# Six transformer layers on one core: when the next layer's weights and tables are fetched, Newton's temporaries in PSUM, and the order of k's transfers

## The chip, the core and the metric

The kernel runs on one core of a Trainium2 chip. Its engines work side by side and in their own order: PE (TensorE, matmuls; PEld is its weight loading), DVE (VectorE), ACT (ScalarE), POOL (GpSimd, which works on SBUF only here) and SP (SyncE, which issues the DMAs). SBUF is the working memory; PSUM is the small memory that matmuls write, in banks of 512 floats per partition. The metric is the time of one execution in microseconds of the device. Three runs of the kernel before gave 3605.53, 3603.47 and 3618.85 us, median 3605.53.

## The reference

The input has 16 sequences of 256 tokens with 128 features, all float32. First a plain causal attention with 16 heads of 8 is added to x. Then come six layers (the Stack), whose result is added to x:

```python
for i in range(DEPTH):                     # 6
    x = attn_layer(shift_tokens(x), Wqkv[i], q_scale[i], k_scale[i], Wo[i]) + x
    x = ffn_layer(shift_tokens(x), ln_g[i], ln_b[i], W1[i], b1[i], W2[i], b2[i]) + x
```

`attn_layer` has 16 heads of 64. It projects q, k and v, normalizes q and k of each head to length 1 and scales them, turns them by rotary tables that also carry a power of the position, and attends in windows: each window of 32 queries sees its own 32 keys and the 32 before, with a mask. `ffn_layer` is a layer norm, a product with W1 (128 x 682), one half times the gelu of the other, and a product with W2 (341 x 128). `shift_tokens` moves half of the features by one token.

## The kernel before

The first stage computes the plain attention and its residual in about 390 us; nothing of it is changed. The second stage is the Stack. All activations stay in SBUF as `yT`, features on partitions and two sequences of 256 tokens side by side. One step n = 16 l + s is layer l with sequence s, so n runs from 0 to 95. Each step is written as two halves, u = 0 and u = 1, for the first and second half of the heads, and in one half the pieces of several steps are interleaved:

- of step n + 2: q and k are projected by `proj_qk` (L484 to L504) for group g of four heads, k = 0 for q and 1 for k. Two matmuls (L497) write one PSUM bank, ACT squares it (L498, `sq`), and DVE multiplies it with the rotary table `ab` (L499, `t`, 128 x 1024). POOL adds the squares (`add_sq`, L509) and the turned halves (`add_t`, L515, `tq`).
- of step n + 1: `norms` sums squares by matmul, `roots` (L530 to L547) transposes the sums into PSUM (`nT`, L533) and DVE takes the inverse square root of 128 x 64 numbers: a lower bound (L537, `nx`), a first guess by an integer trick (L541, `rn`), and three Newton rounds of three instructions (L544 to L546, temporaries `nz`). POOL spreads the result (`spread_rn`, L552, `kb`), PE transposes it into PSUM (`spread_k`, L563, `bc`), DVE multiplies k by it (`norm_k`, L577), and SP sends q and k of two groups to `us` (L579): per group, one transfer for each u.
- of step n: `masks` writes the mask into the PSUM tile `simt` with one ACT copy of 128 x 1024 (L604), `sim` adds the scores with 128 matmuls (L617), `soften` scales them and takes the maximum on DVE (L629, L637), `below` subtracts it on POOL (L643, `sm`), `power` is the exponential on ACT (L648, `ex`). `proj_v` (L587) makes v, ACT copies it to `vn` (L593) and SP sends shifted copies to `vs` (L594, L596).
- of the half before: `share` and `divide_by` make the weights sum to one (L655, L656; L664 on POOL, and on DVE for the second part of the first heads), `attn_T` transposes them (L670, L672, `aT`), `attn_v` multiplies with v (L690), `evict` copies the result (L701).
- of step n - 1: `project_out` multiplies with Wo (L712) and DVE adds to `yT` (L717). The feed-forward part of a pair of steps is spread over four halves.

`ORDER` names the pieces of the four kinds of half (even or odd step, u = 0 or 1), and `in_order` pins the sequence of instructions on PE, DVE, ACT and POOL to it. The order of DMAs on SP is the planner's: it puts a load into the queue as soon as its buffer is free. Small PSUM tiles come from one pool of four banks (`psum1`); the planner gives out the banks. The tiles `wqk` (one for each g), `wv`, `wout`, `w1`, `w2` exist once; `ab` and the tag `t12` have two buffers, `tq` six.

Weights are asked for at a layer's first use of them: `proj_qk` with s == 0 and k == 0 calls `load_qk` (L429) and, for g == 0, `load_tables`, which fetches the rotary table (L437) and multiplies it with the layer's scales by two POOL instructions of 128 x 1024 (L439). They stand in POOL's order at this place, the piece Q0a of the half with n + 2 = 16 l and u = 0, behind SM0 and SM1 (L664) and ahead of QA0 (L509), QT0 (L515), SB0, SB1 (L643) and KB (L552). `proj_v`, `project_out` and `glu_part` call `load_v`, `load_out` and `load_glu` in the same way.

Of the kernel before, what the change touches and what calls it, by code (L numbers as in the profile page):

```python
# [7 lines left out]
F32 = mybir.dt.float32  # L8
# [30 lines left out]
def tile_transformer(  # L39
# [347 lines left out]
    with ExitStack() as st:  # L387
# [59 lines left out]
        def load_v(l):  # L447
            W["v"] = wpool.tile([P, 2, NG, 2, DH], F32, tag="wv", name=f"wv_{l}")
            src = f_wqkv[l][:, 2 * INNER :].rearrange("p (g u y) -> p u g y", g=NG, u=2)
            for u in range(2):  # L450
                nc.sync.dma_start(W["v"][:, u].rearrange("p g x d -> p g (x d)"), src[:, u])

        def load_out(l):

            w = wpool.tile([P, 2, 4, E], F32, tag="wout", name=f"wout_{l}")
            for x in range(2):
                for g in range(2):
                    nc.sync.dma_start(
                        w[64 * x : 64 * x + 64, g],
                        f_wo[l].rearrange("(g x i d) e -> g x d i e", g=2, x=2, i=4, d=DH)[g, x],  # L460
                    )
            W["out"] = w

        def load_glu(l):
            w1 = wpool.tile([P, 2 * DI], F32, tag="w1", name=f"w1_{l}")
            nc.sync.dma_start(w1, f_w1[l])
            w2 = wpool.tile([P, 3, E], F32, tag="w2", name=f"w2_{l}")
            for i, (a, n) in enumerate(DI_PARTS):
                nc.sync.dma_start(w2[:n, i, :], f_w2[l][a : a + n, :])
            W["1"], W["2"] = w1, w2  # L470

        xs, sq2s, t12s, sq, tq, us, rn, kbs, ao, exs, aTs, pos, xns, hs = ({} for _ in range(14))
# [11 lines left out]
        def proj_qk(n, g, k):  # L484

            l, s = divmod(n, NSEQ)
            if s == 0 and k == 0:
                load_qk(l, g)
                if g == 0:
                    load_tables(l)  # L490
            if k == 0:
                sq2s[n, g] = e2.tile([P, 2, 2, S], F32, tag="sq2", name=f"sq2_{n}_{g}")
                t12s[n, g] = e2.tile([P, 2, 2, 2, S], F32, tag="t12", name=f"t12_{n}_{g}")
            sq2, t12 = sq2s[n, g], t12s[n, g]
            ps = psum1(f"qk_{n}_{g}_{k}")
            for t in range(2):
                nc.tensor.matmul(ps[:, t * S : t * S + S], W["qk", g][:, k, t, :], xs[n], start=True, stop=True)  # L497
            nc.scalar.activation(sq2[:, k].rearrange("p t n -> p (t n)"), ps, AF.Square)  # L498
            nc.vector.tensor_tensor(  # L499
                t12[:, k].rearrange("p f t n -> p f (t n)"),  # L500
                ps.unsqueeze(1).to_broadcast([P, 2, 2 * S]),
                W["ab", l][:, k].rearrange("p f t n -> p f (t n)"),
                ALU.mult,
            )  # L504
# [25 lines left out]
        def roots(n, n2):  # L530
            ps = psum1(f"nT_{n}").rearrange("p (h g m) -> p h g m", h=4, g=4)
# [4 lines left out]
            x = p2.tile([P, 2, NG, 8], F32, tag="nx", name=f"nx_{n}")  # L536
            nc.vector.tensor_scalar(x, ps[:, 0:2, :, 0:8], 1e-24, None, ALU.max)  # L537

            y = p3.tile([P, 2, NG, 8], F32, tag="rn", name=f"rn_{n}")
            x_, y_ = (v.rearrange("p h g m -> p (h g m)") for v in (x, y))  # L540
            nc.vector.tensor_scalar(y_.bitcast(I32), x_.bitcast(I32), -0.5, 1597463007.0, ALU.mult, ALU.add)  # L541
            for _ in range(3):
                z = p4.tile([P, 64], F32, tag="nz", name=f"nz_{n}")
                nc.vector.tensor_tensor(z, x_, y_, ALU.mult)  # L544
                nc.vector.scalar_tensor_tensor(z, z, -0.5, y_, ALU.mult, ALU.mult)
                nc.vector.scalar_tensor_tensor(y_, z, 1.5, y_, ALU.add, ALU.mult)  # L546
# [20 lines left out]
        def norm_k(n, j):  # L567
# [4 lines left out]
            ps = bcs.pop((n, j))  # L572
            for a in range(2):
                g = 2 * j + a
                t4 = tq.pop((n, g))
                k = t4[:, :, 1]
                nc.vector.tensor_tensor(k, k, ps[:, a].unsqueeze(1).to_broadcast([P, 2, S]), ALU.mult)  # L577
                for u in range(2):
                    nc.sync.dma_start(us[n, u][:, g], t4[64 * u : 64 * u + 64])  # L579

        def proj_v(n, u, c):

            l, s = divmod(n, NSEQ)
            if u == 0 and c == 0 and s == 0:
                load_v(l)
            ps = psum1(f"v_{n}_{u}_{c}")
            nc.tensor.matmul(  # L587
                ps, xs[n][:, P * c : P * c + P], W["v"][:, u].rearrange("p g x d -> p (g x d)"), start=True, stop=True
            )
            v, w = vn[u], vs[u]  # L590
# [7 lines left out]
        def masks(n, u):  # L598

            if n == 0 and u == 0:  # L600
                for x in range(2):
                    nc.tensor.matmul(simt[:, x], ident_b, mask_s, start=True, stop=True, skip_group_check=True)
            else:
                nc.scalar.copy(simt, mask_s.unsqueeze(1).to_broadcast([P, 2, 512]))  # L604
# [54 lines left out]
        def divide_by(n, i):  # L659
# [3 lines left out]
            on = nc.vector if i == 1 else nc.gpsimd  # L663
# [39 lines left out]
        def project_out(n, u):  # L703

            l, s = divmod(n, NSEQ)
            if s == 0 and u == 0:
                load_out(l)
            a = ao.pop((n, u))
            ps = psum1(f"wo_{n}_{u}")
            for j in range(4):  # L710
                g, x = divmod(j, 2)
                nc.tensor.matmul(  # L712
                    ps[:, :S].rearrange("p (h m) -> p h m", h=2), W["out"][:, g, 2 * u + x, :], a[:, x, :, g, :],
                    start=(j == 0), stop=(j == 3)
                )
            y = yT[s // 2][:, (s % 2) * S : (s % 2 + 1) * S].rearrange("p (a h m) -> p h a m", a=2, h=2)
# [85 lines left out]
        def glu_part(mm, i):  # L802
            l, b, _, w, name = which(mm)
            if b == 0 and i == 0:
                load_glu(l)
# [11 lines left out]
            hs[mm, i] = h  # L817

        def glu_out(mm):
            l, b, c0, w, name = which(mm)  # L820
            ps = psum1(f"w2_{name}")[:, :w]
# [3 lines left out]
            nc.vector.scalar_tensor_tensor(y, ps, vecs[:, l, V_B2 : V_B2 + 1], y, ALU.add, ALU.add)  # L825

# [25 lines left out]
        def sums(n):  # L852
# [3 lines left out]
            (0, 0): "SH0 SM0 SH1 SM1 S0 S1 Q0a Q0b QA0 QT0 NS S2 S3 SO0 SB0 SO1 SB1 WO RT KB AT0 AT1 V0 AV0 AC0 MK Q1a GP2 Q1b QA1 QT1 SK0 NK0 PW0 PW1 AV1 AC1 V1",  # L856
            (0, 1): "SH0 SM0 SH1 SM1 S0 S1 Q0a Q0b QA0 QT0 SK1 NK1 S2 S3 SO0 SB0 SO1 SB1 WO SHF GS AT0 AT1 V0 AV0 AC0 MK Q1a Q1b QA1 QT1 PW0 PW1 AV1 AC1 GO V1",
            (1, 0): "SH0 SM0 SH1 SM1 S0 S1 Q0a Q0b QA0 QT0 NS S2 S3 SO0 SB0 SO1 SB1 WO RT KB AT0 AT1 V0 AV0 AC0 MK GC Q1a GV Q1b QA1 QT1 GT SK0 NK0 PW0 PW1 AV1 AC1 V1",
            (1, 1): "SH0 SM0 SH1 SM1 S0 S1 Q0a Q0b QA0 QT0 SK1 NK1 GN S2 S3 SO0 SB0 SO1 SB1 WO SHF AT0 AT1 V0 AV0 AC0 MK Q1a GP0 GP1 Q1b QA1 QT1 PW0 PW1 AV1 AC1 V1",
        }  # L860

        def half(n, u):
# [16 lines left out]
            def roots_of(n):  # L879
# [5 lines left out]
                "SM0": lambda: do(b, divide_by, bi),  # L885
                "SM1": lambda: do(b, divide_by, bj),
# [14 lines left out]
                "RT": lambda: do(n + 1, roots_of),  # L901
                "SK0": lambda: do(n + 1, spread_k, 0),
# [15 lines left out]
                "MK": lambda: do(*((n, masks, 1) if u == 0 else (n + 1, masks, 0))),  # L918
# [12 lines left out]
            if n == N - 1 and u:  # L931
                what["WO"] = lambda: (do(n - 1, project_out, u), glu_shift((N // 2 - 1, 0)))
# [3 lines left out]
        def tail():  # L936
# [5 lines left out]
            for i in (2, 3):  # L942
                share(n, i)
                divide_by(n, i)
# [4 lines left out]
            project_out(n, 0)  # L949
            for i in (2, 3):  # L950
# [5 lines left out]
            project_out(n, 1)  # L956
            glu_shift(z)
# [122 lines left out]
```

## Time and profile before

| | |
|---|---|
| median of three runs | 3605.53 us |
| the profiled execution, by the device | 3608.32 us |
| its span, first to last instruction | 3606.5 us |
| mean granted TensorE clock | 0.989 |
| DMA queue q1: packets, MB | 248060, 321.14 |
| L499 `t`, DVE | 768 of 1217 ns |
| L439 `ab`, POOL | 12 of 1896 ns |
| L604 mask, ACT | 191 of 1022 ns |
| L544, L545, L546 (Newton), DVE | 288 each, mean 478, 333, 230 ns |
| L541 (first guess), DVE | 96, mean 415 ns |

How to read it: the profile records one execution. Busy time is the time in which an engine has an instruction at work; "idle before" is the time the engine stood still ahead of an instruction, with the event that ended it. `out<-in` names tiles without buffer numbers: `qk`, `nT`, `bc`, `v`, `hg`, `ha`, `cen` and others are PSUM tiles of the pool of four. A wait is put down to the last event before the instruction, so a name may be that of a neighbour. PEclk is the granted clock of TensorE, 1.00 being full speed.

### The profile page before, as it was taken

To read this page: it belongs to the slowest core of one execution; us is meant where nothing else is said; L and a number is where in the kernel's file an instruction comes from. 1 tells how busy PE (TensorE), PEld (TensorE's weight loads), DVE (VectorE), ACT (ScalarE), POOL (GpSimd) and SP (SyncE) were. 2 spreads that over 40 slices of the span, in tenths; PEclk is the share of its full clock that TensorE was granted. 3 is DMA by queue.
4 is the path that set the end of the run, shared out by engine and by line. 5 is a ranking of instruction groups with operands and counts; after the bars stand their busy time and mean duration, and the time that the engine had idled before them with its cause. 6 is when DMAs were issued, how large, how long until landed. Compare 5 with 4: busy or idle time off the path is not lost.

```text
span 3606.5 us, 151183 instructions
## 1 busy us (share of the span) xinstructions
PE 3435.6 (95%) x66566; PEld 2405.9 (67%) x66567; DVE 2840.4 (79%) x4876; ACT 2031.6 (56%) x3377; POOL 2576.9 (71%) x2730
## 2 busy tenths in 40 slices
PE   7999699999999999999999999999999999999997
PEld 6777466666666666666666666666666666666665
DVE  5665788887888887877887888887888888888784
ACT  3444355655665655655655655655656565565554
POOL 2221788777777787777777777777787877777772
PEclk9999899999999999999999999999999999999999
DMA  3000333334443334333334333334433343343332
GB/s 83 10 9 10 93 94 99 101 93 108 112 106 88 90 103 117 94 102 99 80 103 118 104 91 100 101 94 110 111 95 84 100 113 91 104 106 101 92 106 60
DMA packets 249436, 331.51 MB, mean 92 GB/s; under 512 B 74446, under 2 KB 105548, under 8 KB 247884
## 3 DMA queue, kind: packets, MB, share of 16 engines
q1 hardware_dynamic: 248060, 321.14, 33.9%
q8 instruction: 525, 8.60, 1.0%
q14 instruction: 131, 1.07, 0.1%
q10 hardware_dynamic: 720, 0.70, 0.1%
HBM read 28.14 MB, written 4.19 MB: 9 GB/s over the span
## 4 chain that ended last, share of the span: by engine, by line
PE 55%; DVE 21%; ACT 8%; issue 8%; POOL 4%; DMA 3%; SPq 0%; DVEq 0%; POOLq 0%; ACTq 0%
PE qk L497 12%; PE po L690 9%; PE v L587 7%; DVE t L499 7%; PE wo L712 5%; PE simt L617 5%; PE w L823 4%; DVE tq L577 3%; PE ha L810 2%; PE hg L809 2%; DMA vs<-vn 2%; DVE rec L655 2%; ACT simt L604 2%; DVE mx L637 2%; PE aT L670 2%
## 5 line engine op out<-in xcount | busy, mean ns | idle before, releaser
L499 DVE TENSOR_TENSOR t<-qk,ab 128x1024 f32<-128x1024 f32 x768 | 911.7, 1217 | 306.1 <-ACT sq L498 235.2
L515 POOL TENSOR_TENSOR tq<-t 128x512 f32<-128x512 f32 x768 | 961.5, 1273 | 99.8 <-DVE t L499 63.7
L497 PE MATMUL qk<-xs,wqk 128*128 128x256 f32 x3072 | 792.5, 394 | 0.3 <-DVE tq L577 0.2
L509 POOL TENSOR_TENSOR sq<-sq 128x512 f32<-128x512 f32 x384 | 498.9, 1299 | 330.2 <-ACT sq L498 318.9
L497 PEld LDWEIGHTS qk<-xs,wqk 128*128 128x128 f32 x3072 | 555.4, 191 | 154.6 <-issue 31.8
L498 ACT ACTIVATE sq<-qk 128x512 f32<-128x512 f32 x768 | 454.2, 599 | 222.9 <-PE qk L497 221.3
L672 ACT COPY aT<-aT 128x512 f32<-128x512 f32 x384 | 210.3, 587 | 604.0 <-PE aT L670 603.1
L587 PE MATMUL v<-wv,xs 128*128 128x512 f32 x768 | 429.0, 641 | 46.8 <-DVE tq L577 22.5
L690 PEld LDWEIGHTS po<-aT,vs 64*64 64x64 f32 x12288 | 329.2, 135 | 207.3 <-issue 142.2
L643 POOL TENSOR_TENSOR sm<-sm,mx 128x512 f32<-128x512 f32 x384 | 396.1, 1044 | 28.3 <-DVE mx L637 27.0
L690 PE MATMUL po<-aT,vs 64*64 64x32 f32 x12288 | 397.1, 223 | 9.9 <-DMA vs<-vn 5.6
L617 PEld LDWEIGHTS simt<-us 64*32 64x32 f32 x24576 | 261.7, 106 | 206.4 <-issue 196.5
L690 PE MATMUL po<-aT,vn 64*64 64x32 f32 x12288 | 389.1, 220 | 4.0 <-issue 4.0
L593 ACT COPY vn<-v 128x512 f32<-128x512 f32 x384 | 225.4, 587 | 295.8 <-PE v L587 294.2
L712 PE MATMUL wo<-ao,wout 128*128 128x256 f32 x1536 | 382.7, 392 | 0.0
L690 PEld LDWEIGHTS po<-aT,vn 64*64 64x64 f32 x12288 | 331.8, 136 | 4.2 <-issue 4.2
L617 PE MATMUL simt<-us 64*32 64x64 f32 (+1 forms) x24576 | 324.4, 222 | 2.6 <-DMA us<-tq 2.4
L664 POOL TENSOR_TENSOR ex<-ex,rec 128x512 f32<-128x512 f32 x288 | 296.7, 1045 | 35.6 <-DVE rec L656 18.3
L712 PEld LDWEIGHTS wo<-ao,wout 128*128 128x128 f32 x1536 | 276.0, 189 | 47.4 <-issue 0.4
L701 ACT COPY ao<-po 128x512 f32<-128x512 f32 x384 | 223.6, 582 | 126.9 <-PE po L690 126.4
L637 DVE TENSOR_REDUCE mx<-sm 128x8 f32<-128x512 f32 x384 | 263.5, 686 | 13.3
L655 DVE TENSOR_REDUCE rec<-ex 128x8 f32<-128x512 f32 x384 | 252.0, 656 | 25.2 <-ACT ex L648 25.2
(147 smaller groups left out, 5321.2 us busy)
## 6 DMA issues: line engine op xcount, KB each, us to landing
us<-tq SPq DMA_DIRECT2D x768, 256.0 KB
vs<-vn SPq DMA_DIRECT2D x384, 192.0 KB
vs<-vn SPq DMA_DIRECT2D x192, 64.0 KB
wqk<-in_f_wqkv_dram SPq DMA_DIRECT2D x96, 64.0 KB
ab<-in_tables_dram SPq DMA_DIRECT2D x6, 1024.0 KB
wv<-in_f_wqkv_dram SPq DMA_DIRECT2D x12, 256.0 KB
wout<-in_f_wo_dram SPq DMA_DIRECT2D x24, 128.0 KB
x<-in_x_dram SPq DMA_DIRECT2D x16, 128.0 KB
```

The lines of the kernel that those rows point to most:

```text
L497: nc.tensor.matmul(ps[:, t * S : t * S + S], W["qk", g][:, k, t, :], xs[n], start=True, stop=True)
L498: nc.scalar.activation(sq2[:, k].rearrange("p t n -> p (t n)"), ps, AF.Square)
L499: nc.vector.tensor_tensor(t12[:, k].rearrange("p f t n -> p f (t n)"), ps.unsqueeze(1).to_broadcast([P, 2, 2 * S]), W["ab", l][:, k].rearr ...
L509: nc.gpsimd.tensor_tensor(sq[n, g], sq2[:, :, 0, :], sq2[:, :, 1, :], ALU.add)
L515: nc.gpsimd.tensor_tensor(tq[n, g][:, t], t12[:, :, 0, t, :], t12[:, :, 1, 1 - t, :], ALU.add)
L587: nc.tensor.matmul(ps, xs[n][:, P * c : P * c + P], W["v"][:, u].rearrange("p g x d -> p (g x d)"), start=True, stop=True)
L617: nc.tensor.matmul(ps[WIN * r : WIN * r + WIN, x, col + first : col + 64], qk[part, g, 0, WIN * c : WIN * c + WIN], qk[part, g, 1, WIN * ( ...
L637: nc.vector.tensor_reduce(mx, seg, AX.X, ALU.max)
L643: nc.gpsimd.tensor_tensor(seg, seg, mx.unsqueeze(2).to_broadcast([P, 8, 64]), ALU.subtract)
L655: nc.vector.tensor_reduce(rec, seg, AX.X, ALU.add)
L690: nc.tensor.matmul(po[DH * y : DH * y + DH, h, x, g, WIN * r : WIN * r + WIN], v[64 * h : 64 * h + 64, r // 2, 2 * g + y, x, :], aT[64 * h ...
L712: nc.tensor.matmul(ps[:, :S].rearrange("p (h m) -> p h m", h=2), W["out"][:, g, 2 * u + x, :], a[:, x, :, g, :], start=(j == 0), stop=(j == 3)
```

## The change

1. Loads. Except for the first layer, each weight is asked for right behind the last instruction of the layer before that reads it: `load_qk(l + 1, g)` after the second matmul pair of group g in step s = 15, and so on. `wv` and `wout` are split into a tile for each u, `load_glu` into `load_glu1` and `load_glu2`; `wout` comes in eight transfers a layer in place of four. `load_tables(l + 1)`, the fetch and the two POOL products, is called at s = 8 of layer l, in the piece Q0a.
2. Newton. The lower bound `x_` and the temporary `z` are columns 256 to 383 of the PSUM tile `nT`, in place of SBUF tiles. `y_` stays in SBUF. The tile `nT` is therefore read and written up to the last Newton round.
3. Transfers. `norm_k` multiplies both groups first; then SP gets the two transfers for u = 0 and after them the two for u = 1.
4. Masks. One ACT copy for both halves of `simt` becomes two copies of 128 x 512, called MK0 and MK1.
5. The functions `rotate`, `newton` and `add_out` hold what stood at the end of `proj_qk`, `roots` and `project_out`. `ORDER` calls them right behind what they were cut from, so that the order on the engines stays. `divide_by` gets its engine as an argument; it is the same as before in every half.

```diff
         def proj_qk(n, g, k):
 
             l, s = divmod(n, NSEQ)
-            if s == 0 and k == 0:
+            if n == 0 and k == 0:
                 load_qk(l, g)
                 if g == 0:
                     load_tables(l)
+            if s == NSEQ // 2 and g == k == 0 and l + 1 < DEPTH:
+                load_tables(l + 1)
...
+            qkps[n, g, k] = ps
+            if s == NSEQ - 1 and k == 1 and l + 1 < DEPTH:
+                load_qk(l + 1, g)
+
+        def rotate(n, g, k):
+
+            ps = qkps.pop((n, g, k))
             nc.vector.tensor_tensor(
-                t12[:, k].rearrange("p f t n -> p f (t n)"),
+                t12s[n, g][:, k].rearrange("p f t n -> p f (t n)"),
                 ps.unsqueeze(1).to_broadcast([P, 2, 2 * S]),
-                W["ab", l][:, k].rearrange("p f t n -> p f (t n)"),
+                W["ab", n // NSEQ][:, k].rearrange("p f t n -> p f (t n)"),
                 ALU.mult,
             )
...
-            x = p2.tile([P, 2, NG, 8], F32, tag="nx", name=f"nx_{n}")
-            nc.vector.tensor_scalar(x, ps[:, 0:2, :, 0:8], 1e-24, None, ALU.max)
+
+        def newton(n):
+
+            room = nTs.pop(n)
+            ps = room.rearrange("p (h g m) -> p h g m", h=4, g=4)
+            x_, z = (room[:, 256 + 64 * k : 320 + 64 * k] for k in range(2))
+            nc.vector.tensor_scalar(
+                x_.rearrange("p (h g m) -> p h g m", h=2, g=NG), ps[:, 0:2, :, 0:8], 1e-24, None, ALU.max
+            )
...
             nc.vector.tensor_scalar(y_.bitcast(I32), x_.bitcast(I32), -0.5, 1597463007.0, ALU.mult, ALU.add)
             for _ in range(3):
-                z = p4.tile([P, 64], F32, tag="nz", name=f"nz_{n}")
                 nc.vector.tensor_tensor(z, x_, y_, ALU.mult)
                 nc.vector.scalar_tensor_tensor(z, z, -0.5, y_, ALU.mult, ALU.mult)
                 nc.vector.scalar_tensor_tensor(y_, z, 1.5, y_, ALU.add, ALU.mult)
...
+            t4s = [tq.pop((n, 2 * j + a)) for a in range(2)]
             for a in range(2):
-                g = 2 * j + a
-                t4 = tq.pop((n, g))
-                k = t4[:, :, 1]
+                k = t4s[a][:, :, 1]
                 nc.vector.tensor_tensor(k, k, ps[:, a].unsqueeze(1).to_broadcast([P, 2, S]), ALU.mult)
-                for u in range(2):
-                    nc.sync.dma_start(us[n, u][:, g], t4[64 * u : 64 * u + 64])
+            for u in range(2):
+                for a in range(2):
+                    nc.sync.dma_start(us[n, u][:, 2 * j + a], t4s[a][64 * u : 64 * u + 64])
...
-        def masks(n, u):
+        def masks(n, u, x):
...
-                nc.scalar.copy(simt, mask_s.unsqueeze(1).to_broadcast([P, 2, 512]))
+                nc.scalar.copy(simt[:, x], mask_s)
```

## The prediction

> **What bounds the kernel now.** I read the busy table and the slices first, then cut the second stage (the Stack, from 394 us) into its 192 halves, each counted from its first simt matmul (L617), with the table of busy times by window (length, then busy time of each engine, PE's granted clock, DMA share, GB/s), and then read the timeline of single halves: start, us, instruction, and in brackets the idle time before it and what ended it.
>
> ```profile
> PE 3435.6 (95%) x66566; PEld 2405.9 (67%) x66567; DVE 2840.4 (79%) x4876; ACT 2031.6 (56%) x3377; POOL 2576.9 (71%) x2730
> ...
> PE   7999699999999999999999999999999999999997
> ...
> 1182.88:1199.10 16.22, 15.98 (x319) 10.91 (x318) 14.15 (x27) 11.30 (x18) 12.71 (x13) 1.00 0.11 31
> 1199.10:1215.32 16.22, 15.59 (x304) 10.91 (x303) 13.27 (x20) 8.74 (x16) 14.05 (x19) 1.00 0.60 161
> 1215.32:1231.53 16.21, 15.74 (x327) 10.94 (x326) 13.29 (x27) 9.20 (x17) 12.35 (x12) 1.00 0.11 31
> 1231.53:1248.26 16.73, 16.73 (x310) 11.61 (x309) 13.56 (x20) 9.97 (x15) 12.47 (x14) 1.00 0.58 156
> 1379.38:1399.69 20.31, 16.23 (x319) 10.85 (x318) 14.44 (x28) 12.78 (x20) 17.22 (x15) 1.00 0.28 84
> ```
>
> The four kinds of half take 16.22, 16.22, 16.21 and 16.73 us, of which PE is busy for 15.98, 15.59, 15.74 and 16.73: PE sets the time, and a repeating set of four leaves 0.24 + 0.63 + 0.47 + 0 = 1.34 us to gain. The last row is the half in which a new layer's first q and k are projected: 20.31 us with the same PE work. There are five of these (20.28, 20.32, 20.31, 21.59, 20.30 us), together 21.7 us over 16.22 each. The idle rows of one say why:
>
> ```profile
> 1383.98 3.76 POOL L439 TENSOR_TENSOR ab<-ab,qks 128x1024 f32<-128x1024 f32 x2
> ...
> 1385.92 1.23 DVE L499 TENSOR_TENSOR t<-qk,ab 128x1024 f32<-128x1024 f32 x1 [4.22 <-POOL ab L439]
> ...
> 1387.20 0.66 PE L670 MATMUL aT<-cst,ex 128*128 128x128 f32 x4 [1.15 <-DVE t L499]
> 1389.05 0.66 PE L670 MATMUL aT<-cst,ex 128*128 128x128 f32 x4 [1.19 <-DVE t L499]
> ...
> 1397.02 0.63 PE L563 MATMUL bc<-cst,kb 128*128 128x128 f32 x4 [1.74 <-POOL kb L552]
> ...
> 1377.36 2.03 SPq L429 DMA_DIRECT2D wqk<-in_f_wqkv_dram  x4
> 1379.49 0.45 SPq L437 DMA_DIRECT2D ab<-in_tables_dram  x1
> ```
>
> The wait is not for weights. The last four pieces of wqk are issued at 1377.36, just after the last qk matmul of the old layer (1376.73 to 1377.33), and the first four at 1348.86, behind matmuls that ended at 1348.82: SP already sends them right behind the last use, and no PE wait names them. The table `ab` of a layer is issued some 500 us before its use (851.6, 1379.5, 1915.1, 2444.9 us). What is late is the scaling of the table on POOL (L439, two of 1.9 us): DVE's t waits for it, PE for the PSUM banks that t frees (1.15 + 1.19), and the delay reaches kb through DVE's Newton (1.74).
>
> **The change, part by part.** The sum is made against the profiled execution, 3608.3 us (span 3606.5, 1.8 around it); the median of the runs is 3605.5, 2.8 less.
>
> **Loads.** Moving them to the last use removes no PE wait, since none is there: 0. wout comes in 8 pieces a layer and not 4; SP issues these at about 0.65 us each on a queue that mostly waits (0 on PE; bound +2 us at the start of the Stack, where the loads stand close before the first us transfers).
>
> **Tables at s = 8.** This is what the first part really does. The two products leave the layer's first half: t then waits for its square alone, and the five halves fall to 16.22: **-21.7 us**. They run instead six sequences into each of the first five layers, at the same place in POOL's queue, behind the two ex and ahead of sq. Behind them wait sq, two tq, two sm and kb. In the ordinary half, from its start, the second ex ends at 4.65; then 3.76 (products), 1.27 (sq), 2.50 (tq), 2.04 (sm) and 1.04 (kb), with 0.04 to 0.05 of overlap at each seam, put kb's end at 15.08. Today kb ends at 13.39 and bc starts at 13.54 with no PE idle. So bc starts at about 15.2 and PE idles 1.66 us, five times: **+8.3 us**. Bounds: 0, if PE had that slack, and 5 x 3.76 = 18.8, if POOL's delay passed on whole.
>
> **The clock.** Five PE stops of 1.3 to 1.7 us with no releaser stand in the trace. Those of 1.68 (1610.8) and 1.59 (1679.9) are followed by 3.4 us at half clock, in which `w` took 4.54 us in place of 2.84; the one of 1.33 (2211.2) and the 1.74 above are not. I take two in five for the new stops, 1.7 us each: **+3.4** (0 to 8.5). [...]
>
> **Newton in PSUM.** The same 11 DVE instructions, each on 64 elements. Now they run 224 ns when alone, but wait for POOL:
>
> ```profile
> L544 DVE TENSOR_TENSOR nz<-nx,rn x288: 224/225/1223, 385.8 to 3519.1; 128x64 f32<-128x64 f32 x144
> L545 DVE SCALAR_TENSOR_TENSOR nz<-nz,rn x288: 224/226/970, 386.1 to 3519.4; 128x64 f32<-128x64 f32 x144
> ...
> L537 DVE TENSOR_SCALAR nx<-nT x96: 211/215/224, 385.2 to 3516.5; 128x64 f32<-128x64 f32 x96
> L541 DVE TENSOR_SCALAR rn<-nx x96: 195/493/1067, 385.4 to 3516.7; 128x64 int32<-128x64 int32 x96
> ```
>
> The columns of ns are least, median, most. The instructions with two SBUF inputs, and the SBUF copy-like L541, reach 1 us; L537, which reads PSUM, never leaves 211 to 224, and the others with one PSUM input (L629 676 to 692, L577 677) don't either. With a PSUM operand in each, I expect 11 x 0.22 + 10 x 0.035 = 2.8 us in place of 4.3 (1190.78 to 1195.10), and DVE loses (137.8 - 64.5) + (95.9 - 64.5) + (66.3 - 64.5) + (39.8 - 20.6) = 126 us of busy time. No DVE write to PSUM is in the trace; ACT's mask (1022 ns for 1024 into PSUM) lies on the line of its copies out of PSUM (372 for 256, 587 for 512), so I take no extra price, between 0 and one more 215 each. On the path this is worth **0** in the steady state: t of the next product starts at 1195.05, and its square ended at 1194.95, so t would not start earlier; KB ends earlier, but bc had no idle. At the start of the Stack it counts: there bc waits for kb, kb for Newton, by 5.40, 3.39, 2.06 and 1.05 us in the first four sequences (Newton 4.35 and 6.13 in the first two). I take **-4** (0 to -11.9). The price is room: the bank of nT is held to the end of Newton, 2.6 us more, with four banks in all. The next allocations are v (takes the bank of the first aT, 0.24 idle today), then qk or cen, hg or qk, and so on; two banks (wo, freed at 1190.86, the second aT at 1191.10) are free before qk at 1192.78, and v's at 1192.41 before ha at 1194.61: 0.
> [...]
>
> **Masks.** One ACT copy of 1024 (1022 ns) becomes two of 512. The ACT rows (372 at 256, 587 at 512) give 0.84 ns an element and 0.16 us fixed; the next starts 0.10 before the end of the one before. So +0.06 us for each half. Behind it wait sq, then t, tq and the banks for v (even sequences), and fsq, then pv, on which PE idles 0.23 (odd): 2 x 0.06 x 48 = **+5.8** (0 to 15, without the overlap).
>
> **Order of us.** The same eight transfers, u = 0 first. In the half from 1199.10 they are issued 0.4 to 9.6 us after its start, for simt matmuls 16 us after it or later; PE waits for us only at the start (2.4 us in all). A tq buffer is released one issue later (0.7 us), and POOL's next tq then has 0.9 us of slack before sm: 0.
>
> **Sum.** -21.7 + 8.3 + 3.4 - 4 + 5.8 = -8.2; 3608.3 - 8.2 = 3600.1, and with the 2.8 by which the median lies below, **3597.5 us**, 0.2% faster. What a measurement of this kernel can tell from no change is 0.5%, 18 us, so the forecast is no difference.
>
> **The rivals.**
> 1. The moved products are covered: if sq and tq let kb through (their readers come a half later, but the order is fixed) or PE arrives late anyhow, 8.3, 3.4 and 5.8 vanish: 3605.5 - 21.7 - 4 = 3580, faster. For it: POOL idles 2.03 before kb. Against it: 3.76 is more than that. Chance 0.12.
> 2. The bank of nT, the slower side: if the planner gives it to the next qk in even sequences (needed at 1192.78, Newton ends at 1190.78 + 2.8 = 1193.6), PE stops 0.8 us, 48 times: +38, so 3597.5 + 38 = 3636. It decides as soon as Newton ends later than 2.0 us after its start and the bank goes to that qk. For it: only four banks, and PE idles 0.24 to 0.63 at v for banks already. Against: two others are free earlier. Chance 0.10.
> 3. The layer's first half stays long, because what I read as the table is really the burst of loads: then -21.7 falls away: 3597.5 + 21.7 = 3619. For it: five transfers are issued within 4 us before the stop. Against: the DVE row names the product. Chance 0.08.
> The forecast has 0.70.
>
> **How the numbers follow.** With all bounds of the terms at one end the forecast would be 3572 (-33.6) or 3626 (+20.6); most of it lies well inside. Faster takes rival 1 and little else: 0.13. Slower by over 0.5% (above 3623.6) takes rival 2 and a part of rival 3: 0.13. Same: 0.74. The range for 8 in 10 reaches to the edge of rivals 1 and 3: 3582 to 3619.
>
> **What would show it.** Right: the five halves at a layer's start at 16.2 us with no DVE wait for `ab`; five halves in mid-layer at 17.9 to 19.6 with bc waiting for kb; nz groups at a mean of 220 to 240 ns and DVE busy near 2715; two mask copies of 0.59; shorter bc waits before 510 us. Wrong: nz over 350 ns, qk or hg waiting for rn, or steady halves that differ from 16.22 by over 0.15.

## The result, and the profile after

| | before | changed |
|---|---|---|
| median (8 runs each, the same chip) | 3609.75 us | 3630.66 us |
| lowest to highest | 3603.47 to 3618.85 | 3625.06 to 3641.32 |
| the profiled execution | 3608.32 us | 3641.32 us |
| its span | 3606.5 us | 3639.5 us |

The ratio is 1.0056, with a 95% interval of 1.0040 to 1.0072 (it is not simply the quotient of the medians): the change makes the kernel slower by 0.6%. Forecast were 3597.5 us and "no difference", with a range of 3582 to 3619. The profiled execution of the changed kernel is the longest of its eight, 10.7 us above the median, so that its parts add up to +33 us, and not to the 20.9 between the medians.

The busy table and PE's slices of the changed kernel:

```profile
PE 3446.4 (95%) x66567; PEld 2406.3 (66%) x66567; DVE 2724.8 (75%) x4876; ACT 2059.8 (57%) x3568; POOL 2572.0 (71%) x2730
...
PE   7999799999999999999999999999999999999997
```

DVE lost 115.6 us of busy time and ACT has 191 instructions and 28 us more; nothing here tells where time was lost. That is seen when halves are compared with their counterparts. (odd, u1) below is the half u = 1 of an odd step, and so on; u0 halves are those of both kinds of step. The busy times by window of the changed kernel, columns as before: the four kinds of half, a half at a layer's start, and the mid-layer half with the products and the one behind it.

```profile
1190.49:1206.91 16.42, 16.06 (x320) 10.92 (x319) 12.74 (x27) 11.47 (x19) 12.72 (x13) 1.00 0.11 30
1206.91:1223.12 16.21, 15.73 (x303) 10.99 (x302) 13.25 (x20) 8.79 (x17) 13.12 (x19) 1.00 0.69 161
1223.12:1239.53 16.41, 15.74 (x327) 10.94 (x326) 12.30 (x28) 9.35 (x18) 12.94 (x12) 1.00 0.11 31
1239.53:1256.47 16.94, 16.90 (x310) 11.58 (x309) 13.56 (x20) 10.12 (x16) 12.40 (x14) 1.00 0.64 154
1389.08:1405.50 16.42, 16.06 (x319) 10.91 (x319) 12.73 (x27) 11.46 (x19) 12.72 (x13) 1.00 0.34 104
1124.12:1141.88 17.76, 16.09 (x319) 10.92 (x318) 14.07 (x29) 12.73 (x21) 17.65 (x16) 1.00 0.10 28
1141.88:1157.13 15.25, 15.25 (x303) 10.86 (x303) 12.02 (x18) 7.63 (x14) 12.49 (x18) 1.00 0.73 171
```

The layer's start is now an ordinary half, as forecast. But the ordinary halves, some 48 of each kind, are not what they were: the u0 halves take 16.42 and 16.41 us in place of 16.22 and 16.21, (even, u1) stays at 16.21, and (odd, u1), 16.73 before, takes 16.94 in the row shown; most of these are longer, their median is 17.39. All halves, changed less before, from the two profiles (medians are of the differences, half by half):

| | us |
|---|---|
| first sim of the Stack: 394.23 to 399.06 | +4.8 |
| halves of the first four sequences | -8.5 |
| five layer-start halves, 20.3 to 16.42 | -20.7 |
| five mid-layer halves, 16.22 to 17.77, and the five behind them | +7.7, -6.2 |
| other u0 halves, +0.197 each (82) | +14.9 |
| other (odd, u1) halves, median +0.43 (45) | +25.9 |
| other (even, u1) halves, median +0.006 (41) | +15.5 |
| end | -0.3 |

In the five mid-layer halves the products push kb back, and PE stops for 1.43 to 1.45 us ahead of bc. PE's row names DVE's `h`, but its weight load waits for kb, and in e3 below, where the squares come earlier again, both name kb:

```profile
1128.73 3.74 POOL L439 TENSOR_TENSOR ab<-ab,qks 128x1024 f32<-128x1024 f32 x2
...
1138.09 1.03 POOL L571 COPY kb<-rn 128x1024 f32<-128x1024 f32 x1
...
1139.17 0.42 PEld L582 LDWEIGHTS bc<-cst,kb 128*128 128x128 f32 x4 [1.83 <-POOL kb L571]
1139.18 0.66 PE L582 MATMUL bc<-cst,kb 128*128 128x128 f32 x4 [1.43 <-DVE h L841]
```

The row of the halves behind them holds two long ones of before (19.79 and 17.85 us) and one of the changed kernel (18.93); the other four of the changed kernel take 15.24 to 15.43 us. The (even, u1) sum comes from few halves, most of them with a PE stop of 1.5 to 2.1 us at `po`, once at `w`, for which the profile names no releaser. Such halves are in the profile of before too (19.89 and 19.31 us, and the two above). The same sum is between -4.2 and +3.3 us in the profiles of single parts below, but +4.6 to +11.7 in e1 to e4. I read it as chance, and as a good part of the 10.7 us by which this execution is long; no run shows that. Two rows carry the question: the u0 halves and the (odd, u1) halves. A few waits answer to the latter. From the lists of the costliest groups (the first row from the longer list, with three releasers), before and then changed (busy us and mean ns, then idle us before it with its releasers):

```profile
L515 POOL TENSOR_TENSOR tq<-t 128x512 f32<-128x512 f32 x768 | 961.5, 1273 | 99.8 <-DVE t L499 63.7 <-DMA us<-tq 23.1 <-DVE tq L577 3.7
...
L690 PE MATMUL po<-aT,vs 64*64 64x32 f32 x12288 | 397.1, 223 | 9.9 <-DMA vs<-vn 5.6
```

```profile
L527 POOL TENSOR_TENSOR tq<-t 128x512 f32<-128x512 f32 x768 | 961.2, 1273 | 146.8 <-DMA us<-tq 67.3
...
L709 PE MATMUL po<-aT,vs 64*64 64x32 f32 x12288 | 397.3, 222 | 24.5 <-DMA vs<-vn 19.7
```

PE now waits 19.7 us for the shifted copies `vs`, 5.6 before; and POOL waits 67.3 us for the transfers that read `tq`, 23.1 before. Both point to the transfers of `us`.

### The profile page after: what moved, and what is told of

It reads as the page before. It is cut to its first block, busy times and chain, and to the rows that moved or that the text cites. A ratio compares the mean times of both kernels' runs of the same rounds, so it can differ in the third digit from the quotient of the medians.

```text
span 3639.5 us, 151134 instructions
## 1 busy us (share of the span) xinstructions
PE 3446.4 (95%) x66567; PEld 2406.3 (66%) x66567; DVE 2724.8 (75%) x4876; ACT 2059.8 (57%) x3568; POOL 2572.0 (71%) x2730
## 4 chain that ended last, share of the span: by engine, by line
PE 56%; DVE 18%; issue 9%; ACT 8%; DMA 5%; POOL 4%; SPq 1%; DVEq 0%; POOLq 0%; ACTq 0%
PE qk L502 13%; PE po L709 8%; PE v L606 7%; DVE t L511 6%; PE simt L637 5%; PE wo L731 4%; PE w L854 4%; DMA vs<-vn 4%; PE ha L837 3%; PE hg L836 3%; DVE tq L595 2%; ACT simt L624 2%; DVE mx L657 2%; ACT sq L503 2%; PE aT L689 2%
## 5 line engine op out<-in xcount | busy, mean ns | idle before, releaser
L527 POOL TENSOR_TENSOR tq<-t 128x512 f32<-128x512 f32 x768 | 961.2, 1273 | 146.8 <-DMA us<-tq 67.3
L709 PE MATMUL po<-aT,vs 64*64 64x32 f32 x12288 | 397.3, 222 | 24.5 <-DMA vs<-vn 19.7
L683 POOL TENSOR_TENSOR ex<-ex,rec 128x512 f32<-128x512 f32 x288 | 296.4, 1043 | 46.2 <-DVE rec L676 20.9
```

Source lines behind the costliest of these rows:

```text
L527: nc.gpsimd.tensor_tensor(tq[n, g][:, t], t12[:, :, 0, t, :], t12[:, :, 1, 1 - t, :], ALU.add)
L683: on.tensor_tensor(seg, seg, rec.unsqueeze(2).to_broadcast([P, 8, 64]), ALU.mult)
L709: nc.tensor.matmul(po[DH * y : DH * y + DH, h, x, g, WIN * r : WIN * r + WIN], v[64 * h : 64 * h + 64, r // 2, 2 * g + y, x, :], aT[64 * h ...
```

## The experiments

Times are medians; every ratio is to the kernel before on the same chip, with its 95% interval. e1 to e4 ran on one chip (before: 3603.39 us), e5 to e8 on another (3606.74 us), and e9 to e12 ran together too (3605.85 us).

### Undo the masks, undo the order of us, undo both

e1 goes back to one mask copy:

```diff
-            else:
-                nc.scalar.copy(simt[:, x], mask_s)
+            elif x == 0:
+                nc.scalar.copy(simt, mask_s.unsqueeze(1).to_broadcast([P, 2, 512]))
```

e2 goes back to the transfers by group, e3 does both:

```diff
-            for u in range(2):
-                for a in range(2):
+            for a in range(2):
+                for u in range(2):
                     nc.sync.dma_start(us[n, u][:, 2 * j + a], t4s[a][64 * u : 64 * u + 64])
```

> The changed kernel with one mask copy of 1024 in place of two of 512. Theory M (the two copies take 1.21 us from first start to last end in place of 1.02, and ACT's next square, then t, bc and pv, come 0.20 us later): the ordinary halves with u = 0 fall from 16.42 and 16.41 to 16.22 and 16.21, the odd ones with u = 1 lose 0.2 of their excess, in all about -25 us to -29 us: some 3603. Rival (the u = 0 halves wait for something else of the change, a PSUM bank held by Newton): they stay at 16.4 and the time at 3630.

> The changed kernel with the us transfers by group again (u = 0 and u = 1 of the first group, then of the second). Theory T (the order is what makes vs land late, so that PE stops at po in the odd halves with u = 1): these halves fall from 17.1 to 17.8 to a steady 16.93, and the PE idle time at po for vs falls from 15.1 us in all to about 3; the time falls by 12 to 18 us, to some 3615. Rival (vs is late through the loads or the bank of nT): no change within 3 us.

> Both undone: what is left are the loads, the tables at s = 8 and Newton in PSUM. Theories M and T together: all four kinds of half at 16.22, 16.22, 16.21 and 16.73; then -20.7 at the five layer starts, +7.7 at mid-layer less what the next half gives back, -8.5 in the first four sequences, +4.8 at the start of the Stack: about -17 against the kernel before, 3593, 0.995 to 0.996 of its time. If the effects of masks and order overlap (one hides the other), the sum of e1's and e2's gains is larger than what this run gains.

| | us | ratio | u0 halves | (odd, u1) halves | packets, ns | PE at po for vs |
|---|---|---|---|---|---|---|
| changed | 3630.66 | 1.0056 [1.0040, 1.0072] | +0.197 | +0.43 | 147, 145 | 19.7 us |
| e1 | 3603.53 | 1.0001 [0.9990, 1.0012] | 0.00 | +0.25 | 147, 146 | 17.4 us |
| e2 | 3614.15 | 1.0028 [1.0015, 1.0041] | +0.197 | +0.195 | 128, 127 | 7.2 us |
| e3 | 3587.27 | 0.9964 [0.9950, 0.9977] | 0.00 | 0.00 | 127, 125 | 7.2 us |

(Halves: median against before, in the profiles. Packets: mean time of the packets of 2,048 bytes that start within 6 us of the half's first transfer of `us`, in (even, u1) and (odd, u1) halves; before it is 127 and 127. The expectations give 115 and 102 in place of 127, 134 and 119 in place of 147 and 145: means over another choice of packets, with nearly the same ratio.) The two edits that the prediction priced at +5.8 and 0 cost all that was lost, and more: without them the rest of the change is worth -0.4%, and the median of every ordinary kind of half is that of before. Undoing the masks gains 0.55%, undoing the order 0.28% and undoing both 0.92%, so neither hides the other.

### The masks alone, and as two tiles

e9 puts the two copies alone into the kernel before.

```diff
-                nc.scalar.copy(simt, mask_s.unsqueeze(1).to_broadcast([P, 2, 512]))
+                nc.scalar.copy(simt[:, x], mask_s)
...
-                "MK": lambda: do(*((n, masks, 1) if u == 0 else (n + 1, masks, 0))),
+                "MK0": lambda: do(*((n, masks, 1, 0) if u == 0 else (n + 1, masks, 0, 0))),
+                "MK1": lambda: do(*((n, masks, 1, 1) if u == 0 else (n + 1, masks, 0, 1))),
```

> The kernel before with one part of the change alone: two mask copies of 128 x 512 in place of the one of 128 x 1024, on ACT at the same place. All work is kept. Theory: the parts that cost time do not depend on the others. Every ordinary u0 half gets 0.20 us longer (mask, then the square, t, the banks and bc or pv come 0.20 later), and the (odd, u1) halves 0.15 to 0.25: 82 x 0.20 + 45 x 0.2 = 25 us, ratio 1.006 to 1.008. Rival: the copies cost this only together with Newton's earlier end or the moved products: ratio 1.000 to 1.004.

It took 3635.78 us, 1.0082 [1.0069, 1.0095]. The u0 halves are 0.195 and 0.197 longer, (odd, u1) 0.193, (even, u1) 0.00. Why 0.20, where 0.06 was forecast? ACT's timeline in an ordinary u0 half, first of the kernel before, then of the changed one (start, us, instruction; x2 is two in a row):

```profile
1193.40 1.02 ACT L604 CAST simt<-mask_s 128x1024 f32<-128x1024 bf16 x1
1194.35 0.60 ACT L498 ACTIVATE sq<-qk 128x512 f32<-128x512 f32 x1
```

```profile
1201.01 1.22 ACT L624 CAST simt<-mask_s 128x512 f32<-128x512 bf16 x2
1202.16 0.59 ACT L503 ACTIVATE sq<-qk 128x512 f32<-128x512 f32 x1
```

The square follows 0.95 us behind the mask's start before, and 1.15 now. Each copy takes 0.59 us, as forecast; but the second starts 0.03 us after the first one's end (all 191 times), where other ACT instructions in a row mostly overlap by 0.06 to 0.12. The second copy waits on a semaphore that ACT itself raises. Both copies write the one tile `simt`, in different columns; if what is ordered is the tile and not its columns, two tiles should free the second copy. e12 makes two tiles of it:

```diff
-        simt = ps_m.tile([P, 2, 512], F32, name="simt")
+        simt = [ps_m.tile([P, 512], F32, name=f"simt{x}") for x in range(2)]
...
-                nc.scalar.copy(simt[:, x], mask_s)
+                nc.scalar.copy(simt[x], mask_s)
```

> The changed kernel, with simt as two PSUM tiles of one bank instead of one tile of two banks; still two mask copies, nothing else. All work is kept. Theory: the second copy waits for the end of the first because both write one tile (the instruction waits on ACT's own semaphore), so that it starts 0.03 us after its end; with two tiles it starts 0.06 to 0.10 before the end, as other copies in a row do. The squares behind it come 0.10 to 0.13 earlier: the u0 halves are 0.07 to 0.10 us over 16.22 instead of 0.20, and the whole is 8 to 15 us shorter than the changed kernel: ratio 1.001 to 1.004. Rival: two copies into PSUM do not overlap whatever their tiles: the gap stays at 0.03 and the ratio at 1.0045 to 1.007.

```profile
1193.88 1.11 ACT L624 CAST simt<-mask_s 128x512 f32<-128x512 bf16 x2
1194.92 0.60 ACT L503 ACTIVATE sq<-qk 128x512 f32<-128x512 f32 x1
```

The two copies overlap by 0.08, the square follows 1.04 behind the start, the u0 halves are 0.09 over before instead of 0.20, and the time is 3611.46 us, 1.0012 [1.0002, 1.0023]. So in these runs what is ordered is the tile, and of the 0.20 in the u0 halves about half is the wait of the second copy for the first; the other half, 0.09 (1.11 us in place of 1.02), stays with two copies. The prediction's estimate of 0.16 us fixed for each copy, less the overlap of 0.08, comes near it. How much of the 0.44% between e12 and the changed kernel is this wait is less clear, since whatever else waits for `simt` waits for one tile of two there as well.

The (odd, u1) halves pay because they have no slack at all: the square is 0.20 later, so is DVE's `t` (11.41 us after the half's start before, 11.61 in e9), and PE's second `ha`, which the profile lets wait for `t`, starts 12.88 us after the half's start where it started at 12.69; from there on everything in the half is 0.19 later. The (even, u1) halves absorb it in their 0.63 us of PE idle.

### The order of us alone, and crossed

e10 puts the order alone into the kernel before; e4 is the changed kernel with the order (u0, group a), (u1, group b), (u0, b), (u1, a), in which neighbours read different halves of the partitions, while each `tq` is still released late.

```diff
-            for u in range(2):
-                for a in range(2):
-                    nc.sync.dma_start(us[n, u][:, 2 * j + a], t4s[a][64 * u : 64 * u + 64])
+            for u, a in ((0, 0), (1, 1), (0, 1), (1, 0)):
+                nc.sync.dma_start(us[n, u][:, 2 * j + a], t4s[a][64 * u : 64 * u + 64])
```

> The kernel before with one part of the change alone: after both products with k, SP gets the two transfers for u = 0 and then the two for u = 1, so that two transfers in a row read the same 64 partitions. All work is kept. Theory: the packets of that burst get slower (from 115 and 102 ns to some 134 and 119), vs behind them lands late, and PE waits for it at po in the (odd, u1) halves: these get 0.2 us longer or more, all others stay: ratio 1.003 to 1.006. Rival: it is late only because kb and bc come at other times in the changed kernel: ratio 0.999 to 1.002.

> The changed kernel with the us transfers crossed: u = 0 of the first group, u = 1 of the second, u = 0 of the second, u = 1 of the first. As in the change, the second transfer waits for the second group's product and the first group's tile is free only after its second transfer, here the last of the four. Theory T-source (two transfers in a row that read the same 64 partitions drain slower, mean packet 134 and 119 ns against 115 and 102): the sources alternate again, so the packets go back to 115 and 102 ns, vs is in time, and the odd halves with u = 1 fall to 16.93, time 3612 to 3618. Theory T-late (what counts is that the first group's tile and the issue of vs come one place later): as the change or worse, 3630 or more.

e10 took 3622.16 us, 1.0040 [1.0026, 1.0054]; the span of its profile grew by 11.5 us, the (odd, u1) halves by 13.4, all other steady halves by nothing; the packets take 146 and 148 ns, and PE waits 16.6 us for `vs`. e4 took 3619.03 us, 1.0042 [1.0029, 1.0055]: its packets are back at 127 and 126 ns and the wait for `vs` at 7.2 us, while POOL still waits 66.5 us for `tq`. Its (odd, u1) halves are 0.20 over before, which is the masks' part; 10.6 us of it were lost ahead of the first sim, where the planner orders the work anew for every edit. So the later release of `tq` is real, but PE does not pay for it. PE pays for the slower burst. SP's queue in one (odd, u1) half of before, then SP's queue and PE's wait in one of the changed kernel:

```profile
1563.69 3.05 SPq L579 DMA_DIRECT2D us<-tq  x4
1566.83 0.76 SPq L594 DMA_DIRECT2D vs<-vn  x1
```

```profile
1572.57 3.27 SPq L598 DMA_DIRECT2D us<-tq  x4
1575.94 1.05 SPq L615 DMA_DIRECT2D vs<-vn  x1
1578.38 3.64 SPq L598 DMA_DIRECT2D us<-tq  x4
```

```profile
1581.81 0.32 PE L709 MATMUL po<-aT,vs 64*64 64x32 f32 x8 [0.76 <-DMA vs<-vn]
```

`vs` stands behind the four transfers, and these take longer to issue (median 3.30 us, 3.05 before). Each packet of the burst takes some 15% longer (147 and 145 ns, 127 before), so `vs`, behind it, lands late in the one half that has no slack: the waits at po are 0.76 us here, up to 1.01 in others, and 1.28 and 1.77 in two halves of sequence 15, where the load of `wv` stands ahead too. The one of 1.77 and one of 1.88, in the half behind a mid-layer half, were followed by 3.4 us at half clock; these two halves took 20.28 and 18.93 us. In the slow orders (changed, e1, e10) two neighbours read the same 64 partitions, but they also write the same tile `us[n, u]`; in the fast ones (before, e2, e3, e4) neither holds. No run here separates the two.

### The rest of the change, part by part

e7 moves only the tables to sequence 8; e6 has only Newton in PSUM; e8 only the weights' loads behind their last use.

```diff
# e7, on the kernel before
-                if g == 0:
+                if n == g == 0:
                     load_tables(l)
+            if s == NSEQ // 2 and g == k == 0 and l + 1 < DEPTH:
+                load_tables(l + 1)
# e6, on the kernel before
-            x = p2.tile([P, 2, NG, 8], F32, tag="nx", name=f"nx_{n}")
+            x_, z = (room[:, 256 + 64 * k : 320 + 64 * k] for k in range(2))
...
-                z = p4.tile([P, 64], F32, tag="nz", name=f"nz_{n}")
# e8, on e3
-            if s == NSEQ // 2 and g == k == 0 and l + 1 < DEPTH:
-                load_tables(l + 1)
+            if s == g == k == 0:
+                load_tables(l)
...
-            x_, z = (room[:, 256 + 64 * k : 320 + 64 * k] for k in range(2))
+            x_ = p2.tile([P, 64], F32, tag="nx", name=f"nx_{n}")
...
+                z = p4.tile([P, 64], F32, tag="nz", name=f"nz_{n}")
```

> The kernel before with one part of the change alone: from the second layer on the tables' load and products are made at sequence 8 of the layer ahead instead of sequence 0; the weights stay where they were in the kernel before. All work is kept. If the long layer-start halves (20.3 us) come from the products alone, the five fall to 16.3 (-20 us), the five (sequence 6, u0) halves rise by 1.5 us and lend some of it: ratio 0.9945 to 0.997. If the weights' loads at the layer's start had a share in them, the halves stay between 17 and 20 us: ratio 0.998 to 1.002.

> The kernel before with one part of the change alone: Newton's x and z in the free columns of nT's bank; everything else, the issue order too, as before. All work is kept. Theory: it is worth nothing in the steady halves (16.2 to 16.7 us stay), takes 8 to 11 us out of the halves of the first four sequences, where DVE's chain to kb is what bc waits for, and the planner's prelude before the first sim may shift by 0 to 5 us because it sees other costs: ratio 0.997 to 1.000. Rival: the 1.4 us by which kb comes earlier shorten every (even, u0) half by 0.1 us or more: 48 x 0.1 = 5 us more, ratio below 0.997. Rival from the other side: the PSUM operands hold DVE up in the steady halves (DVE is the releaser of sim's and attn's waits): ratio above 1.001.

> One part of the change alone: the next layer's weights (q and k, v, out, both of the GLU) are fetched behind their last use, with the out weights and v in halves; the tables at sequence 0 of the layer, Newton's temporaries in SBUF, the one mask copy and the transfers by group are as in the kernel before (the steps rotate, newton and add_out stay split, which alone changes nothing of the order in the steady halves). All work is kept. Theory: the five layer-start halves stay at 20.3 us, the weights were hidden anyway: ratio 0.999 to 1.001, and if the eight pieces of the out weights hold the first transfers of us up, 2 to 5 us more before the first sim (up to 1.002). Rival: the loads at the layer's start are what made those halves long: they fall to 16 to 18 us, ratio 0.9945 to 0.997.

| | us | ratio | first sim | first four sequences | layer-start halves | mid-layer halves |
|---|---|---|---|---|---|---|
| e7 tables | 3602.92 | 0.9988 [0.9977, 0.9999] | -0.2 | -0.7 | 16.22 (-21.7) | 19.1 to 21.3 (+20.8) |
| e6 Newton | 3600.63 | 0.9982 [0.9973, 0.9992] | +4.6 | -9.2 | 19.3 to 20.0 (-4.2) | 16.22 |
| e8 weights | 3608.85 | 1.0006 [0.9996, 1.0016] | +0.4 | -1.6 | 20.3 to 21.8 (+3.0) | 16.23 |

The weights were hidden; moving them gains nothing, and the (odd, u1) halves of sequence 15, where the load of `wv` now stands ahead of the transfers of `us`, are 17.4 to 17.7 us in e8 (16.7 to 17.3 before), some 3 us in all. The tables did make the layer-start halves long. But e7 missed its expectation: moved alone, they make the mid-layer halves about as long as the layer-start halves were, 20.4 us in the mean where the changed kernel has 17.8. DVE's timeline in such a half of e7, and POOL's:

```profile
1123.12 0.21 DVE L539 TENSOR_SCALAR nx<-nT 128x64 f32<-128x64 f32 x1
...
1123.66 1.22 DVE L546 TENSOR_TENSOR nz<-nx,rn 128x64 f32<-128x64 f32 x1
1124.91 1.19 DVE L547 SCALAR_TENSOR_TENSOR nz<-nz,rn 128x64 f32<-128x64 f32 x1
1126.14 1.19 DVE L548 SCALAR_TENSOR_TENSOR rn<-nz,rn 128x64 f32<-128x64 f32 x1
```

```profile
1123.53 1.28 POOL L511 TENSOR_TENSOR sq<-sq 128x512 f32<-128x512 f32 x1
1124.75 2.50 POOL L517 TENSOR_TENSOR tq<-t 128x512 f32<-128x512 f32 x2
...
1130.50 1.04 POOL L554 COPY kb<-rn 128x1024 f32<-128x1024 f32 x1 [1.25 <-DVE rn L548]
```

The products push `sq` and `tq` on POOL into Newton's time, and three of Newton's instructions with two SBUF inputs then take 1.19 to 1.22 us, about as long as one POOL instruction beside them (1.25 to 1.28), where the last three, with POOL idle, take 0.23; so kb has to wait for Newton. With a PSUM operand in each, the instructions of the three rounds stay at 223 to 233 ns; the rows of the changed kernel (least, median, most ns):

```profile
L563 DVE TENSOR_TENSOR nT<-nT,rn x288: 223/232/233, 384.9 to 3550.4; 128x64 f32<-128x64 f32 x144
L564 DVE SCALAR_TENSOR_TENSOR nT<-nT,rn x288: 223/232/233, 385.1 to 3550.7; 128x64 f32<-128x64 f32 x144
L565 DVE SCALAR_TENSOR_TENSOR rn<-nT,rn x288: 224/224/225, 385.4 to 3550.9; 128x64 f32<-128x64 f32 x144
```

So Newton in PSUM, worth nothing in an ordinary half, is worth 13 us in the five mid-layer halves (+7.8 in e3, +20.8 in e7): without it the move of the tables would only have moved the loss. About half of this is the clock, by an estimate from the lengths of the halves: bc waits 2.81 to 2.83 us for kb in all five halves of e7, four of the stops are followed by 3.4 or 6.8 us at half clock, and these four halves take 20.0 to 21.3 us, the fifth 19.1.

### A better version: the products where GpSimd is idle

In the (odd, u1) halves POOL stands idle for some 3 us behind the shifted copies (2.87 in the one from 1239.53 of the changed kernel). e5 is e3 with the table's load at sequence 5 and one product each behind the copies of sequences 7 and 9; e11 also pins the two halves of step n = -1 to the written order.

```diff
+        def tables_ahead(n):
+            l, s = divmod(n, NSEQ)
+            if l + 1 < DEPTH:
+                if s == 5:
+                    load_tables(l + 1)
+                if s in (7, 9):
+                    scale_tables(l + 1, (s - 7) // 2)
...
-            (1, 1): "... WO WA SHF AT0 ...",
+            (1, 1): "... WO WA SHF TB AT0 ...",
...
-                in_order(traced, n >= 0)
+                in_order(traced, n >= -1)
```

(The last edit is e11's alone.)

> The changed kernel with the one mask copy and the transfers by group, and the next layer's table products moved once more: the table's load at sequence 5 of a layer, and the two products (1.88 us each) singly behind the shifted copies of sequences 7 and 9, in the (odd, u1) halves, where GpSimd stands idle for 2.95 us before it adds the squares. All work is kept. If what the mid-layer products cost is the wait of kb behind them, the five (sequence 6, u0) halves fall from 17.8 us to 16.2, with no half longer in exchange. What that is worth is open between two theories: the half behind such a long half is now shorter by about 1 us, so that the long half is mostly lent (then 5 x 0.6 = 3 us, ratio to the kernel before 0.995 to 0.9965), or the short one behind it is chance (then 8 us, ratio 0.994 to 0.995). If GpSimd's gap is not free (the squares or the sums behind it come late), the (odd, u1) halves of sequences 7 and 9 get longer and the ratio stays at 0.9964 or above.

> The kernel with the tables in GpSimd's gap, one mask copy and the transfers by group, and one line more: the two halves of step n = -1 ahead of the first sim are pinned to the written order too (before, the planner ordered them). All work is kept. Theory: with the cheaper Newton the planner put the sums of a later group ahead of kb on GpSimd, and so the first bc and the first sim came 4.6 to 5.8 us later; pinned, kb goes first: first sim back at 394 to 396 us in the profile, 3 to 6 us less than the kernel with the tables in the gap, ratio 0.9915 to 0.994. Rival: what the prelude gains, the halves of the first four sequences lose again (they were 7.5 to 11 us shorter), since the same work is only moved: ratio 0.9935 to 0.9955.

e5 took 3584.14 us, 0.9938 [0.9924, 0.9953]. A mid-layer half of it, and the half with the first product, 16.22 and 16.73 us like all of their kind:

```profile
1113.26:1129.48 16.22, 15.98 (x319) 10.91 (x318) 12.73 (x27) 11.30 (x18) 12.71 (x13) 1.00 0.11 30
```

```profile
1161.90:1178.63 16.73, 16.73 (x309) 11.61 (x308) 13.56 (x20) 9.96 (x15) 14.34 (x15) 1.00 0.59 156
```

The products cost nothing there. Against e3 the five mid-layer halves are 7.8 us shorter in the profile and the five behind them 4.3 longer: a long half is in good part lent, as the first theory had it, though the ratio alone would have fitted the second. The spans of the two profiled executions are equal (3582.3), since e5's start (up to the first sim, and the first four sequences) is 7.2 us longer, and e3 and e5 ran on different chips; that e5 is better than e3 is not shown. Both are better than the kernel before and the changed one.

e11 took 3586.96 us, 0.9944 [0.9932, 0.9957]. kb does stand ahead of the sums now, yet the first sim comes at 397.9 us (e5 400.1, before 394.2), and the second bc is late instead. The theory that the order of kb alone makes the start late fell. Newton's part alone brings a later start (e6: +4.6), yet e3, which has it too, starts only 2.1 us later; what else in the prelude is late stays open. It costs nothing on balance, since the first four sequences are 6.7 to 11 us shorter.

## Why the prediction was wrong

- **What bounds the kernel**: right, and more strictly than it was used. The table of the four halves showed 0 us of slack in (odd, u1) and 0.24 to 0.63 in the others; two edits were then priced without asking what they do to that half.
- **Loads: 0.** Near: 1.0006 in e8, some 3 us at the ends of layers. The bound of +2 at the start for eight pieces of `wout` is not needed (+0.4).
- **Tables: -21.7 + 8.3.** Right to a microsecond: -20.7 with the masks' 0.20 in each (-21.7 in e3), and +7.7 (+7.8 in e3, without the second mask copy). bc stops PE for 1.43 to 1.46 us, 1.66 was forecast. The chain of POOL to kb was worked out from the rows, and it was free of Newton only because of the other part; the prediction did not see that the two depend on each other. In four of the five cases the half behind was 1 us shorter, which the sum left out.
- **Clock: +3.4.** 0 for the stops it was meant for: none of the five (1.43 to 1.45 us) was followed by half clock. The sample it was taken from was misread: the Stack of before has four PE stops of 1.3 to 1.7 us with no releaser, not five, and half clock stands also behind stops of 1.13 to 1.20 us in three of the five layer-start halves (from 861.2, 2455.2 and 2984.2 us), but not behind those of 1.33 and 1.74. The length of a stop alone does not decide it. Half clock did follow two waits for `vs`, of 1.77 and 1.88 us.
- **Newton: -4.** 11 instructions of 0.23 us, no price for the DVE writes to PSUM, DVE down by 115.6 us (126 forecast). At the start -8.5 for the halves and +4.8 for the first sim, together -3.7; e6 alone took 0.18% less than before, some 6.5 us. The room of nT's bank cost nothing.
- These four terms add up to -14.0; e3, which has them and no more, measured -13.0 (-0.36% of 3603.4, interval -8 to -18; the medians differ by 16.1). That it comes so near is partly luck: the clock's +3.4 was 0, the halves behind the mid-layer halves gave back some 4 us that the sum left out, and the start of e3's profile is 8.9 us shorter.
- **The sum itself**: 3600.1 less 2.8 is 3597.3 and not 3597.5, and the upper bound of 20.6 leaves out the 2 of the loads. Neither matters for the outcome.
- **Masks: +5.8.** The step that failed first. "the next starts 0.10 before the end of the one before" was read from instructions that do not depend on each other; the second copy into `simt` started 0.03 us behind the first one's end, and with two tiles (e12) 0.08 before it. The delay is 0.20 and not 0.06, and it reaches three kinds of half instead of two: (odd, u1) was not in the product 2 x 0.06 x 48. Alone it is +0.8%, some 30 us. The term's upper bound of 15 was for two kinds too.
- **Order of us: 0.** The step that failed second. It asked who waits for `us` and for `tq`; POOL's wait for `tq` did grow, by 44 us in all, but PE does not pay for it (e4). It did not ask what stands behind these transfers in SP's queue. That is `vs`, which PE reads in the half without slack; and it took the transfers to be as fast in any order. Alone it is +0.4%, 14 us.
- **Rivals**: none of the three happened. The slower side came by a mechanism that was not listed, though the last sentence, steady halves off 16.22 by over 0.15, named its sign.

## What to carry to other kernels

Price an edit first in the stretch that has no slack, and follow every queue it touches to what stands behind it, not only to who waits for the moved thing itself. Splitting one copy into two that write one tile cost 0.20 us here (1.22 in place of 1.02); with two tiles it cost 0.09. Parts of a change whose instructions run side by side must be priced together: here one part shortened a wait that the other would have met (bc's for kb, 2.81 to 2.83 us in e7, 1.43 to 1.45 in the changed kernel).

## What the runs showed of the hardware

- Four transfers of 64 partitions each, in one queue: when neighbours read the same 64 partitions (and write the same tile), their packets of 2,048 bytes took 145 to 148 ns (changed kernel, e1, e10), and 125 to 128 ns when they alternated (before, e2, e3, e4).
- Two ACT copies of 128 x 512 into one PSUM tile took 1.22 us (changed kernel), into two tiles 1.11 (e12), one copy of 128 x 1024 1.02 (before).
- Newton's DVE instructions of 64 elements with an operand in PSUM took 0.22 to 0.23 us, also beside POOL's additions (changed kernel); with two SBUF inputs up to 1.22 us beside these additions (e7).
- Half clock of 3.4 or 6.8 us followed four of five PE stops of 2.81 to 2.83 us (e7), and in before pairs of stops of 1.13 to 1.20 us in three of five halves; none of five stops of 1.43 to 1.45 us was followed by it (changed kernel).
